# A second pass with column sums as column tiles, six convolution banks, a set GpSimd order and earlier weight widening

## The chip, the cores and the metric

The kernel runs on one core of a Trainium2 chip. The time is that of one execution on the device, in microseconds (us). The core has five engines that run side by side and wait for each other by semaphores: TensorE (PE, with its weight loads shown as PEld), VectorE (DVE), ScalarE (ACT), GpSimd (POOL) and SyncE (SP), which here issues the DMA transfers. Matrix products are written into PSUM[...]; the other working memory is SBUF.

## The reference

Two layers run over x of shape (8, 256, 64, 64), all in 32-bit floats.

```python
# layer 0: attention of all pixels over keys and values from a 4x4-strided convolution
xr = layernorm_over_channels(conv(x, w_sr, stride=4))
q, (k, v) = w_q @ x, split(w_kv @ xr)
x = x + gamma_s * (w_out @ softmax(q k^T / sqrt(32)) v)          # 8 heads
# layer 1: linear attention over qkv and over a 5x5 depthwise + grouped 8x8 of it
qkv = w_qkv @ x
agg = grouped(w_pw, depthwise5x5(qkv, w_dw))
ms = concat(qkv, agg)                                            # 64 heads of q, k, v with 8 rows
q, k, v = relu(ms.q), relu(ms.k), pad(ms.v, 1.0)                 # a column of ones beside v
kv = k^T v                                                       # per head: 8 x 9
out = q kv;  out = out[:8] / (out[8] + 1e-15)
x = x + batchnorm(w_proj @ out)
```

The ninth column of kv, made by the column of ones, is the sum of k over all pixels. These sums are the "column sums of k" of the title.

## The kernel before

Three passes follow each other in one program. The first pass does layer 0 and the qkv product and stores its results in HBM by planes. The second pass, with which this document deals, does for layer 1 the convolution of q and k and the products k^T v. The third pass divides, projects and adds.

**Units.** The second pass (`second_pass`) runs over 64 units u = (t, k, b): two halves t of the channels, four groups k of 32 channels, eight images b. The depthwise convolution and the small grouped product are one: `factors` loads two factors of the weights (wd and ws) and adds some of them up; `widened_k` and `widened_q` multiply them out into the matrices that PE uses. For k the convolution is done in three parts (`convolve`, i = 2, 0, 1), each of 16 pairs of weight load and product with the full 128x128 array, into one bank tagged cv. `paired` makes their inputs from d, as differences of columns; part 2 has a plain copy on POOL. For q, two units are done together, in nine products (`product`) after `across` and `down` have made differences of columns (c) and rows (y). An even unit does four of the nine, the odd unit after it five. `down` does half of each y on DVE and half on POOL.

**Products.** `summed_raw(u)` multiplies the raw k of unit u (kq) with v; 32 columns of weights at a time, so that four column tiles of the array work side by side on the four 32-partition groups of one bank (tag raw). `summed(p)` does the same for the convolved k of the unit before, p = u - 1, with 288 columns of v at its nine shifts (tag sums); DVE then weighs them with the taps and adds them up (p, kv, mixed, m).

**Column sums.** `reduced` adds up k over its eight parts on POOL in three steps, 512, 256 and 128 columns wide, into red_raw or red_agg. A matmul of one column then adds over the partitions: the reduced k is loaded as full 128x128 weights, and a column of ones runs through. For the raw k this is line 1482, in the raw bank. For the convolved k it is line 1494, in a bank of its own (tag few), called at the end of the unit (`ended`). Each of these is two pairs of load and product in the profile[...]. DVE copies the column beside the other sums, and SP stores both.

**Banks.** cv has five of PSUM's eight banks, raw, sums and few one each. A bank of cv is given back when DVE or ACT has read it.

**Order.** The tile framework sets the order on each engine by a simulation, by priority (the order in which the program text issues instructions) among what is ready in it. `tc.keep_in_program_order` nails one instruction behind the one that was issued before it on its engine. At run time each engine takes its instructions in that order. In the second pass the weight copies and the relu of kq on ACT and most stores on SP are nailed. The instructions of POOL are not, nor those of PE.

**Widening in portions.** The multiplying out of weights is a list of small steps (`chores`), worked off by `do(n)` at fixed places of a unit: before the q products, before convolution part 0, before raw, before convolution part 1 and at the end. The q weights of a group are made in two sets of 18 steps: one on DVE, one on POOL, 16 on ACT (line 613). This happens in the units with b = 1 and 2, called wide here; the first set is used from b = 2 on. Those of k are 32 steps on ACT (line 592), from b = 3 on.

**Start.** Before the loop come `positive(0)` (relu of the first kq on ACT, red_raw of unit 0 on POOL), the loading of the first q factors and the inputs of the first convolution.

The loop's own order for one unit u is: stores; differences of q (even u); convolution part 2; steps; q products; steps; part 0; q products; steps; raw and sums; column sum of raw; steps; part 1; the loads of d for u + 2; column sum of the convolved k; q products; relu of the next kq; steps.

## Time and profile before

| what | value |
|---|---|
| median of three runs | 3558.71 us (3556.86 to 3560.86) |
| the profiled execution | 3560.51 us; span of its instructions 3558.6 us |
| instructions | 91293 |
| L1372, convolution of k on PE | 3072 products, 385.7 us busy |
| L1403, q products on PE | 1536 with y, 512 with c, 256 with d |
| L1458, sums on PE | 4096 products, 265.8 us busy |
| L1441, raw on PE | 4096 products, 49.5 us busy |
| L1482 and L1494, column sums on PE | 128 products each, 24.5 and 18.4 us busy |
| L1352 to L1354, reduction on POOL | 64 each of red_raw and red_agg, 1.3, 0.8 and 0.5 to 0.7 us each |
| L613, widening of q on ACT | 256 copies, 0.34 us each |
| PE's idle time between 1960 and 2961 us | 23.5 us |
| DMA | 647 MB; from 1985 to 2800 us 260 GB/s |

Lines are those of the kernel before, and times within a trace count from the span's start. In the lines of the profile a group is named by line, engine, operation and tiles (out<-in), with "128*32" for the rows and columns of the array that a matmul uses. In the view in order of time the first two numbers are start and length in us, and a bracket at the end tells how long the engine was idle before and for whom it waited. A line of the waits reads: who, for whom, us in total, times, the longest. The view of stages gives for each stretch its length and then, for each engine, busy time and instructions. Busy times of PE are modelled where products overlap, so the starts of weight loads are the better measure of its pace. "issue" stands for a wait that the profile attributes to nobody.

### The profile page before, as it was taken

The page shows a single profiled execution, that of the slowest core. Times are in us where ns is not written, and L with a number is a line of the kernel's source. Part 1 is how long each engine was busy: PE and PEld are TensorE (multiplying, and loading weights), DVE is VectorE, ACT ScalarE, POOL GpSimd, SP SyncE. Part 2 cuts the span into 40 slices and gives each one's busy share as a digit, 9 for nine tenths or more (in the row PEclk, how much of TensorE's full clock was granted, in tenths as well). Part 3 has the DMA queues.
Part 4 walks back from the last instruction along what each step waited for, and adds up shares of the span by engine and source line. Part 5 has one row for each costly group of instructions (what it writes and reads, how often), then busy time and mean ns, then how long its engine had stood idle before and what let it go on. Part 6 is the DMA issues. An engine that isn't in the chain of part 4 may idle for free.

```text
span 3558.6 us, 91293 instructions
## 1 busy us (share of the span) xinstructions
PE 3481.9 (98%) x38050; PEld 2111.5 (59%) x38050; DVE 2278.5 (64%) x3499; ACT 1478.1 (42%) x3385; POOL 1858.6 (52%) x1762
## 2 busy tenths in 40 slices
PE   8999999999999999999998999999999999999998
PEld 5554655545545555455445888888888863333333
DVE  1567476575674766756777777777777774544442
ACT  2345354453453544545553344444444423333322
POOL 3557465565574655655763566555656532222222
PEclk9999999999999999999999999999999999999999
DMA  5446445455364454553646999999899987877873
GB/s 174 114 107 164 125 102 170 115 140 150 101 169 121 104 168 115 141 149 104 176 114 180 260 260 259 266 262 257 251 264 259 270 238 204 239 225 220 233 213 90
DMA packets 577191, 647.26 MB, mean 182 GB/s; under 512 B 81664, under 2 KB 452864, under 8 KB 576768
## 3 DMA queue, kind: packets, MB, share of 16 engines
q1 hardware_dynamic: 576768, 641.34, 64.7%
q8 instruction: 300, 4.92, 0.6%
q14 instruction: 123, 1.01, 0.1%
HBM read 389.85 MB, written 249.23 MB: 180 GB/s over the span
## 4 chain that ended last, share of the span: by engine, by line
PE 88%; DMA 5%; DVE 3%; ACT 1%; POOL 1%; issue 1%; SPq 1%; POOLq 0%; DVEq 0%; ACTq 0%
PE qkv L994 16%; PE p L1799 11%; PE cv L1372 8%; PE sc L847 8%; PE av L879 7%; PE cv L1403 6%; PE o L947 6%; PE q L829 6%; PE sr L750 6%; PE sums L1458 6%; PE rep L1785 2%; DMA raw<-planes 2%; PE av L905 2%; PE raw L1441 1%; PE den L1766 1%; DMA vq<-v 1%
## 5 line engine op out<-in xcount | busy, mean ns | idle before, releaser
L860 ACT ACTIVATE e<-sc 128x512 f32<-128x512 f32 x1024 | 528.4, 604 | 508.9 <-PE sc L847 508.9
L899 POOL TENSOR_TENSOR ef<-ef,e 128x512 f32<-128x512 f32 x512 | 687.8, 1353 | 91.4 <-ACT e L860 68.3
L892 POOL TENSOR_TENSOR ef<-e 128x512 f32<-128x512 f32 x256 | 329.3, 1305 | 544.6 <-ACT e L860 544.5
L1809 POOL TENSOR_TENSOR y<-z,xs 128x512 f32<-128x512 f32 x128 | 165.5, 1302 | 460.8 <-ACT z L1807 460.8
L1372 PE MATMUL cv<-w,c 128*128 128x128 f32 x3072 | 385.7, 279 | 6.3 <-DVE stage L1007 4.0
L1372 PEld LDWEIGHTS cv<-w,c 128*128 128x128 f32 x3072 | 363.1, 194 | 7.7 <-issue 4.1
L847 PE MATMUL sc<-q,kk 32*64 32x256 f32 x8192 | 298.5, 387 | 5.6 <-ACT e L860 5.2
L994 PE MATMUL qkv<-differences,combined 128*128 128x512 f32 x576 | 288.7, 592 | 0.6 <-POOL differences L964 0.6
L926 DVE STREAM_TRANSPOSE rden<-av 128x256 f32<-128x256 f32 x256 | 99.8, 428 | 283.2 <-ACT att L917 235.8
L1458 PE MATMUL sums<-vq,r 128*32 128x288 f32 x4096 | 265.8, 408 | 0.4 <-issue 0.4
L1799 PE MATMUL p<-raw,wp 128*128 128x512 f32 x512 | 248.8, 608 | 9.0 <-ACT z L1807 8.9
L1389 ACT ACTIVATE r<-s 128x512 f32<-128x512 f32 x128 | 80.9, 632 | 413.3 <-DVE s L1388 408.4
L879 PE MATMUL av<-e,vv 64*32 64x256 f32 x8192 | 252.4, 379 | 0.0
L847 PEld LDWEIGHTS sc<-q,kk 32*64 32x64 f32 x8192 | 155.4, 131 | 162.9 <-issue 101.4
L750 PE MATMUL sr<-x,wsr 128*128 128x256 f32 x1024 | 235.6, 382 | 8.7 <-DMA wsr<-in_w_sr_dram 8.6
L829 PE MATMUL q<-x,wq 128*128 128x512 f32 x512 | 241.9, 594 | 0.0
L1799 PE MATMUL p<-agg,wp 128*128 128x512 f32 x512 | 241.1, 593 | 0.0
L750 PEld LDWEIGHTS sr<-x,wsr 128*128 128x128 f32 x1024 | 194.8, 191 | 64.4 <-issue 38.2
L947 PE MATMUL o<-att,wout 128*128 128x512 f32 x512 | 230.3, 592 | 0.0
L932 DVE TENSOR_TENSOR att<-att,rall 128x512 f32<-128x512 f32 x128 | 217.9, 1702 | 4.4
L1010 DVE TENSOR_TENSOR whole<-part,qkv 128x512 f32<-128x512 f32 x256 | 172.3, 683 | 65.9 <-ACT part L1060 49.2
L837 ACT COPY q<-q 128x512 f32<-128x512 f32 x128 | 75.9, 593 | 317.4 <-PE q L829 317.4
(163 smaller groups left out, 6095.8 us busy)
## 6 DMA issues: line engine op xcount, KB each, us to landing
planes<-stage SPq DMA_DIRECT2D x128, 578.0 KB
d<-planes SPq DMA_DIRECT2D x128, 578.0 KB
vq<-v SPq DMA_DIRECT2D x256, 256.0 KB
raw<-planes SPq DMA_DIRECT2D x64, 578.0 KB
x<-in_xp_dram SPq DMA_DIRECT2D x64, 512.0 KB
wsr<-in_w_sr_dram SPq DMA_DIRECT2D x128, 256.0 KB
x<-x SPq DMA_DIRECT2D x128, 256.0 KB
k<-turned SPq DMA_DIRECT2D x256, 128.0 KB
```

What stands on the lines that cost most here:

```text
L750: nc.tensor.matmul(ps[:, oc], w[:, ci, oc * P : (oc + 1) * P], strips(b, f // 2)[:, ci, f % 2 * NK : (f % 2 + 1) * NK], start=(f == ci == ...
L829: nc.tensor.matmul(ps, consts["wq"][:, ci, c * P : (c + 1) * P], strips(b, s)[:, ci], start=(ci == 0), stop=(ci == 1),)
L847: nc.tensor.matmul(scs[h][HALVES[half], QH[kq % 2]], kks[b][rows, c, kq * P // 2 : (kq + 1) * P // 2], qs[rows, QH[half]], start=True, sto ...
L860: nc.scalar.activation(e[:, h % 2].rearrange("p q n -> p (q n)"), scs[h], AF.Exp, scale=D0**-0.5)
L879: nc.tensor.matmul(sums["av"][half][cols, : QB // 2], vvs[b][rows, kq, c * P + h * D0 : c * P + (h + 1) * D0], es[h // 2][rows, h % 2, kq ...
L892: tc.keep_in_program_order(nc.gpsimd.tensor_tensor(f, e[:, :, 0], e[:, :, 1], ALU.add))
L899: tc.keep_in_program_order(nc.gpsimd.tensor_tensor(f, f, e[:, :, half], ALU.add))
L947: nc.tensor.matmul(ps, consts["wout"][:, c, oc * P : (oc + 1) * P], att[c], start=(c == 0), stop=(c == 1))
L994: nc.tensor.matmul(ps, w, x, start=True, stop=True)
L1372: nc.tensor.matmul(ps[:, g * P : (g + 1) * P], c[:, g, cols], w[:, g, n * P : (n + 1) * P], start=(da == 0), stop=(da == 1),)
L1458: nc.tensor.matmul(ps[h * D0 : (h + 1) * D0, : 36 * D1].rearrange("p (r n e) -> p r n e", r=3, e=D1), kt[:, par, h, 2 * r + c], vq[:, r : ...
L1799: nc.tensor.matmul(as_block(ps, i // 2), wp[:, i, oc * P : (oc + 1) * P], block(g, i // 2, i % 2, j), start=(i == 0), stop=(i == 3),)
```

## The change

The column sums are made otherwise. `counted` takes the reduced k in four parts of 32 columns, each to its own column tile of the array, and writes one column per 32 partitions into the bank where the products of the same k already are: column 32 of raw, column 288 of sums. Both are issued one behind the other right after `summed`. The bank few goes away, and cv has six banks. DVE copies the raw sums and their column in one instruction. The work of DVE behind sums moves from `summed` to `ended`, behind the columns.

red_agg of unit p is issued earlier in the text (`reduced_agg`, ahead of convolution part 2 of the next unit). All instructions of POOL in the second pass are nailed: reductions, the copy of part 2, the POOL halves of y, the POOL step of widening.

The steps of widening are done at three places in place of five: 3, 3 and 13 in a wide unit (before 3, 3, 3, 6 and 9), 2, 2 and 4 in others (before four times 2). The last place is ahead of raw. `positive(0)` moves behind the first q factors and the inputs of the first convolution.

```diff
--- before.py
+++ after.py
@@ -600,12 +600,14 @@
     nc = tc.nc
     n = w.shape[1]
     for g in (2, 3):
-        (nc.vector if g == 2 else nc.gpsimd).tensor_tensor(
+        made = (nc.vector if g == 2 else nc.gpsimd).tensor_tensor(
             w[:, :, g].rearrange("p n (o f) -> p n o f", o=D1),
             wd[:, g].unsqueeze(2).to_broadcast([P, n, D1, R * R]),
             ws[:, g].unsqueeze(1).unsqueeze(3).to_broadcast([P, n, D1, R * R]),
             ALU.mult,
         )
+        if g == 3:
+            tc.keep_in_program_order(made)
         yield
     for g in (0, 1):
         for o in range(D1):
@@ -1225,8 +1227,10 @@
     )
     psums = {
         tag: ctx.enter_context(tc.tile_pool(name=f"psum_{tag}", bufs=1, space=bass.MemoryType.PSUM))
-        for tag in ("cv", "raw", "sums", "few")
+        for tag in ("cv", "raw", "sums")
     }
+
+    pinned = tc.keep_in_program_order
 
     def bank(tag, name, bufs=1, n=512):
         return psums[tag].tile([P, n], F32, tag=tag, name=name, bufs=bufs)
@@ -1296,7 +1300,7 @@
         d0, d1, d2 = (d[:, :, :, i : i + NB - 1 : 2] for i in range(3))
         if i == 2:
 
-            nc.gpsimd.tensor_copy(v, d1)
+            pinned(nc.gpsimd.tensor_copy(v, d1))
         else:
             nc.vector.tensor_sub(v, d2 if i else d0, d1)
 
@@ -1322,7 +1326,7 @@
         v = y.rearrange("p i g (b y x) -> p i (g b) y x", b=2, y=NB // 2)
         c0, c1, c2 = (c[:, :, i : i + NB - 1 : 2] for i in range(3))
         nc.vector.tensor_sub(v[:, 0], c0, c1)
-        nc.gpsimd.tensor_tensor(v[:, 1], c2, c1, ALU.subtract)
+        pinned(nc.gpsimd.tensor_tensor(v[:, 1], c2, c1, ALU.subtract))
 
     load_cells(0)
     load_tokens(0)
@@ -1344,14 +1348,14 @@
     ones = const.tile([P, 1], F32, tag="ones", name="ones")
     nc.vector.memset(ones, 1.0)
 
-    kts, reds, raws, mraws, state, maggs = {}, {}, {}, {}, {}, {}
+    kts, reds, raws, mraws, state, maggs, sums = {}, {}, {}, {}, {}, {}, {}
 
 
     def reduced(u, what, t):
         r = mid.tile([P, 4, P], F32, tag=f"red_{what}", name=f"red_{what}_{u}", bufs=1)
-        nc.gpsimd.tensor_tensor(r, t[0], t[1], ALU.add)
-        nc.gpsimd.tensor_tensor(r[:, :2], r[:, :2], r[:, 2:], ALU.add)
-        nc.gpsimd.tensor_tensor(r[:, 0], r[:, 0], r[:, 1], ALU.add)
+        pinned(nc.gpsimd.tensor_tensor(r, t[0], t[1], ALU.add))
+        pinned(nc.gpsimd.tensor_tensor(r[:, :2], r[:, :2], r[:, 2:], ALU.add))
+        pinned(nc.gpsimd.tensor_tensor(r[:, 0], r[:, 0], r[:, 1], ALU.add))
         reds[u, what] = r[:, 0]
 
     def positive(u):
@@ -1364,7 +1368,7 @@
     def convolve(u, i):
         t, k, b = units[u]
         c, w = cells[u, i], wt[t, k]
-        ps = bank("cv", f"cv1_{u}_{i}", 5)
+        ps = bank("cv", f"cv1_{u}_{i}", 6)
         for g in range(4):
             for da in range(2):
                 n = 2 * da + i if i < 2 else 4 + da
@@ -1392,7 +1396,7 @@
     def product(m, i, j):
         t, k, b = units[2 * m]
         now, w = quad[m], wq[t, k, (i, j)]
-        ps = bank("cv", f"cv0_{m}_{i}{j}", 5)
+        ps = bank("cv", f"cv0_{m}_{i}{j}", 6)
         for g in range(4):
             out = ps[:, g * P : (g + 1) * P]
             if i == 1:
@@ -1447,6 +1451,14 @@
                 )
         raws[u] = ps
 
+    def counted(ps, at, red):
+        for j in range(4):
+            cols = slice(j * D0, (j + 1) * D0)
+            nc.tensor.matmul(ps[cols, at : at + 1], red[:, cols], ones, start=True, stop=True)
+
+    def reduced_agg(u):
+        kt = kts[u].rearrange("p q h (n e) -> p q h n e", n=4)
+        reduced(u, "agg", (kt[:, 0].rearrange("p h n e -> p n h e"), kt[:, 1].rearrange("p h n e -> p n h e")))
 
     def summed(u):
         kt, vq = kts.pop(u), vqs.pop(u)
@@ -1462,8 +1474,11 @@
                     start=(i == 0),
                     stop=(i == 7),
                 )
+        sums[u] = ps
+
+    def ended(u):
         t, k, b = units[u]
-        reduced(u, "agg", (kt[:, 0].rearrange("p h n e -> p n h e"), kt[:, 1].rearrange("p h n e -> p n h e")))
+        ps = sums.pop(u)
         p = small.tile([P, 36, D1], F32, tag="p", name=f"p_{u}", bufs=1)
         nc.vector.tensor_mul(p, ps[:, : 36 * D1].rearrange("p (n e) -> p n e", e=D1), taps[t][:, k])
         s = small.tile([P, D1], F32, tag="kv", name=f"kv_{u}")
@@ -1473,26 +1488,18 @@
         nc.vector.tensor_mul(x, mix[:, 4 * t + k], s.unsqueeze(1).to_broadcast([P, D1, D1]))
         m = small.tile([P, D1 + 1], F32, tag="m", name=f"m_{u}")
         nc.vector.tensor_reduce(m[:, :D1], x, AX.X, ALU.add)
+        nc.vector.tensor_copy(m[:, D1:], ps[:, 36 * D1 : 36 * D1 + 1])
         maggs[u] = m
 
     def ended_raw(u):
         t, k, b = units[u]
-        ps = raws.pop(u)
-        col = ps[:, 64:65]
-        nc.tensor.matmul(col, reds.pop((u, "raw")), ones, start=True, stop=True)
         m = small.tile([P, D0 + 1], F32, tag="mraw", name=f"mraw_{u}")
-        nc.vector.tensor_copy(m[:, :D0], ps[:, :D0])
-        nc.vector.tensor_copy(m[:, D0:], col)
+        nc.vector.tensor_copy(m, raws.pop(u)[:, : D0 + 1])
         mraws[u] = m
 
     def stored_raw(u):
         t, k, b = units[u]
         tc.keep_in_program_order(nc.sync.dma_start(kvd[b, t][:, k], mraws.pop(u)))
-
-    def ended(u):
-        col = bank("few", f"few_{u}")[:, :1]
-        nc.tensor.matmul(col, reds.pop((u, "agg")), ones, start=True, stop=True)
-        nc.vector.tensor_copy(maggs[u][:, D1:], col)
 
     def stored_agg(u):
         t, k, b = units[u]
@@ -1529,10 +1536,10 @@
         j = t + 2 * what
         parts[j, k] = factors(nc, kept if what else w_q, a, j, k, 6 if what else 9)
 
-    positive(0)
     load_factors(0, 0)
     for i in (2, 0, 1):
         paired(0, i)
+    positive(0)
     for u in range(n_all + 3):
         p, q = u - 1, u - 2
         now, was, conv = u < n_all, 0 <= p < n_all, 0 <= q < n_all
@@ -1553,6 +1560,8 @@
         if conv and u % 2 == 0:
             across(q // 2, 0)
             down(q // 2, 1)
+        if was:
+            reduced_agg(p)
         if u < 2:
             chores.append(weights_q(0, u))
         if now:
@@ -1575,7 +1584,7 @@
         if u == n_all:
             next(ahead)
         if u == n_all + 1:
-            ahead.send(lambda name: bank("cv", name, 5))
+            ahead.send(lambda name: bank("cv", name, 6))
         if conv and u % 2:
             down(q // 2, 2)
         products(u, 0)
@@ -1588,14 +1597,20 @@
             down(q // 2, 0)
             across(q // 2, 2)
         products(u, 1)
-        do(3 if wide else 2)
+        do(13 if wide else 4)
         if now:
             summed_raw(u)
         if was:
             summed(p)
         if now:
+            counted(raws[u], D0, reds.pop((u, "raw")))
+        if was:
+            counted(sums[p], 36 * D1, reds.pop((p, "agg")))
+        if now:
             ended_raw(u)
-            do(6 if wide else 2)
+        if was:
+            ended(p)
+        if now:
             convolve(u, 1)
         if u + 1 < n_all:
             paired(u + 1, 1)
@@ -1605,14 +1620,11 @@
             load_tokens(2)
         if was and p == n_all // 2 - 1:
             load_taps(1)
-        if was:
-            ended(p)
         products(u, 2)
 
         if u + 1 < n_all:
             positive(u + 1)
-        do(9 if wide else 0)
-    ahead.send(lambda name: bank("cv", name, 5))
+    ahead.send(lambda name: bank("cv", name, 6))
```

## The prediction

> **What bounds the kernel now.** I read the page first, then the stretch of the second pass (about 1927 to 2895 us) in the views of stages, of waits and of time. The page says that TensorE (PE) is busy 98% of the span, and that no other engine comes near; the DMA row is the one to watch beside it.

> ```profile
> PE 3481.9 (98%) x38050; PEld 2111.5 (59%) x38050; DVE 2278.5 (64%) x3499; ACT 1478.1 (42%) x3385; POOL 1858.6 (52%) x1762
> ...
> DMA  5446445455364454553646999999899987877873
> ...
> 1960.00:2961.00 1001.00, 977.48 (x13615) 835.78 (x13610) 749.42 (x1261) 415.15 (x881) 566.49 (x551) 0.99 0.92 258
> ```

> The third line is the stage view over the second pass: length, busy PE, weight loads, DVE, ACT, POOL, then granted clock, DMA share and GB/s. PE has 23.5 us of idle in 1001, weight loads fill 836, and DMA is at 0.92. So a microsecond less of PE work is a microsecond less of time, unless DMA stops it. The order of time shows what one unit's sums cost (weight loads alone):

> ```profile
> 2610.66 0.64 PEld L1441 LDWEIGHTS raw<-vq,kq 128*32 128x32 f32 x63
> ...
> 2611.21 3.57 PEld L1458 LDWEIGHTS sums<-vq,r 128*32 128x32 f32 x63
> 2615.24 0.30 PEld L1482 LDWEIGHTS raw<-ones,red_raw 128*128 128x128 f32 x2 [0.47 <-issue]
> 2615.46 1.87 PEld L1372 LDWEIGHTS cv<-w,c 128*128 128x128 f32 x16
> 2617.24 0.30 PEld L1494 LDWEIGHTS few<-ones,red_agg 128*128 128x128 f32 x2
> 2617.47 0.30 PEld L1403 LDWEIGHTS cv<-y,w 128*128 128x128 f32 x2
> ```

> The reader is to see three spacings: the 64 column-tile pairs of raw take 2611.21 - 2610.66 = 0.55 us (8.6 ns each); L1482 holds PE 0.22 us until the convolution's loads, L1494 0.23; and 0.47 us pass between the loads of sums and L1482. From one L1482 to the next the units take 14.32 and 15.05 us by turns, to 0.01 us, but for one unit in eight. What happens there is in the waits and at 2198 us:

> ```profile
> PE cv L1403 <- ACT w L613: 11.2, 7, 2.3
> PE few L1494 <- POOL red_agg L1354: 4.1, 1, 4.1
> ...
> PE cv L1372 <- DVE s L1388: 1.8, 1, 1.8
> ...
> 2196.53 1.03 ACT L1359 ACTIVATE kq<-kq 128x1024 f32<-128x1024 f32 x1
> ...
> 2197.47 0.81 ACT L613 ACTIVATE w<-wd,ws 128x64 f32<-128x64 f32 x3
> ...
> 2198.33 0.83 PEld L1403 LDWEIGHTS cv<-d,w 128*128 128x128 f32 x6 [1.60 <-ACT w L613]
> ...
> 2437.00:2443.80 6.80, 4.90 (x23) 4.61 (x23) 3.79 (x4) 4.41 (x11) 5.83 (x7) 0.50 0.76 230
> ```

> Seven times PE waits for the last three of 16 weight copies on ACT, which stand behind the next unit's relu (kq). The last line shows the granted clock at 0.50 after two such idles in a row (1.8 and 1.9 us)[...].

> [...] No column tile with one column is in this trace, so I price it as raw's tile of 32. [...] the trace has 0.50 after 2437 and 2563 us, after idles of only about 2 us. [...]

> **The change, part by part.** The sum is made against the profiled execution, 3560.5 us (span 3558.6); the median of the runs is 1.8 lower.

> 1. Column sums. Removed per unit: L1482 0.22 and L1494 0.23, 0.45 us. Added: two times four products of two pairs each, 16 pairs at 8.6 ns = 0.14 us, right behind sums, so in the same tiling. The 0.47 us is mostly the last 288-column products running out: raw, with 32 columns, needs 0.04 from its last load to a full-array load (at 1933.7 us). A part of the new pairs' loads therefore lies in that 0.47. Between the last load of sums and the convolution there are 0.47 + 0.22 = 0.69 us now; I expect 0.47 + 0.14 + 0.04 = 0.65. Gain 0.04 + 0.23 = 0.27 per unit, times 64 = 17.3 us, taken as 17. Bounds: all 16 pairs hidden, 0.36 (23 us); pairs at 12 ns[...], 0.20 (13 us). DVE saves one copy of 0.15 us per unit, which is hidden: it is busy some 11.8 of 15 us.
> 2. Weights sooner. All 18 pieces of a wide unit are now ahead of raw, so the last three no longer stand behind kq; ACT works them off under the 4.6 us of raw and sums (13 x 0.34 = 4.4 us at most; measured spacing 0.26). Five stalled units take 16.00 instead of 14.32 us, 5 x 1.67 = 8.4; the one ending at 2448.96 takes 20.73 (6.4 more, with 1.8 for a bank and half clock), the one ending at 2570.82 18.69 (4.4 more). Together 19.1 us. Late next is the DVE widening (1.24 us) in these units, ahead of the copies that free banks; I leave 1.6 us to it and take 17.5. Bounds: 10 (if the bank wait and the clock drops stay) to 19.
> 3. The sixth bank. Its one visible stall (1.8 us on s, because DVE waited 2.35 us for a load of d) is in the 19.1. Nothing more is counted; PE waits for no other bank in this pass.
> 4. GpSimd in fixed order. POOL is busy 566 of 1001 us. An even unit's queue is now: y from d (2.7, waits for the load of d), red_agg (1.3 + 0.7 + 0.5), copy of c 0.7, perhaps the widening 1.3, y 1.3, red_raw 2.5. Behind a late d stand red_agg, whose column sum PE now needs 2.2 us sooner, and c. At 2612.7 d was in; y ended at 2615.4; r is there at 2620.0, so red_agg would end at 2622.6 and PE asks at 2629.3: 6.7 us to spare. Zero in the steady part. SP's queue gets nothing new; only the store of m waits for a copy behind the same column.
> 5. The start. positive(0) now comes behind the first copy of c, and that copy behind the first pass's last clearing of a stage (ends 1926.2), just before PE's first convolution at 1926.9: nothing. But POOL's first widening, run at 1950.5, now stands ahead of red_raw of unit 1 (run at 1940.1) and red_agg of unit 0 (1937.5). Its factors are issued at 1937.4 to 1939.3; if DVE takes them at 1941 (2.0 us with both engines busy), POOL is through by 1941 + 2.0 + 1.3 + 2.6 + 2.6 = 1949.5, where PE asks at 1944.1: up to 5.4 us, of which a convolution can fill 1.9. Against that goes the wait of 4.1 for few, and the half clock after it. I take a gain of 1; bounds -8 to +5.
> 6. The third pass takes the same bank by another count: zero.

> Sum: 17 + 17.5 + 1 = 35.5 us; 3560.5 - 35.5 = 3525 for a profiled run, 3523 for the median.

> **The rivals.** (a) DMA becomes the bound. For it: share 0.92, and 0.95 from 2760 to 2880 us; at 14.43 instead of 14.90 us per unit it would be 0.95 throughout. Against it: PE waits for DMA only 0.7 us, and 2420 to 2435 shows 1.04. If it holds at 0.94, the pass gains 1 - 0.92/0.94 = 2.1% of 1001, 21 us: 3538. (b) Slower: the fixed POOL order. Decisive where y from d ends more than 6.7 us later than at 2615.4: then red_agg holds PE in the 32 even units, and a stall of 2 us each costs 64 us: 3559 - 35 + 64 = 3588. For it: POOL waits 69.7 us for d, once 11.4. Against: with d that late PE would be waiting for y itself already. (c) The one-column tiles don't run side by side: 16 x 0.11 us (the duration of a 32-column load) = 1.76 per unit, 84 us lost, 3625; slower from 0.72 us per unit on. Raw, with the same tiles, speaks against. (d) The scheduler, which may move PE's work, puts the column sums behind the convolution[...]; some 0.2 per unit, 3527, within the forecast.

> **How the numbers follow.** Forecast with (d) 0.74; (a) 0.12; gains eaten by the start and DMA, no change, 0.04; (b) 0.07; (c) 0.03. About 0.2%, 7 us, can be told from no change. Faster 0.86, same 0.04, slower 0.10. Range: the forecast's terms run from 13 + 10 - 8 = 15 to 23 + 19 + 5 = 47 gained, 3544 to 3512; with 3 us on either side, 3509 to 3547, it holds (a) too.

> **What would show it.** Right: units of 14.05 and 14.78 us by turns, no longer one in eight; loads of the column sums, 128*32, within 0.7 us between sums and the convolution; no wait on w L613; clock 1.00 from 2000 to 2800 us. Wrong: PE waiting for red_agg, red_raw or d in even units; more than 0.3 us from the first load of the column sums to the last; a DMA share over 0.95 with PE idle beside it; DVE's s late by the widening, with PE waiting for it.

## The result, and the profile after

The changed kernel takes 3594.56 us (median of four runs, 3591.53 to 3604.05), and the kernel before, on the same chip, 3558.78 us. The ratio is 1.0102, with a 95% interval of 1.0084 to 1.0120: 36 us slower, where 35 us faster had been forecast. On another chip, in the last series below, it was 1.0103 (1.0080 to 1.0127).

The stage view over the second pass answers to the one shown of before (length, busy PE, weight loads, DVE, ACT, POOL, granted clock, DMA share, GB/s):

```profile
1960.00:2961.00 1001.00, 937.90 (x14360) 824.95 (x14360) 721.01 (x1189) 404.59 (x884) 571.90 (x556) 0.98 0.89 251
```

PE's idle time has grown from 23.5 to 63.1 us, and the DMA share has fallen from 0.92 to 0.89: DMA is not what holds PE. The waits of PE between 1927 and 2895 us tell for whom (who, for whom, us in total, times, the longest):

```profile
PE cv L1407 <- POOL y L1329: 50.5, 29, 3.0
PE raw L1457 <- POOL red_raw L1358: 6.4, 1, 6.4
PE cv L1376 <- DVE stage L1009: 4.0, 1, 4.0
PE sums L1457 <- POOL red_agg L1358: 2.6, 1, 2.6
```

The waits for w (11.2 us before) and few (4.1 us) are gone, as meant. In their place stands a wait that the kernel before does not have: the q products wait for POOL's half of y in almost every even unit. One such unit in the order of time, weight loads alone:

```profile
2271.80 3.57 PEld L1470 LDWEIGHTS sums<-vq,r 128*32 128x32 f32 x63
2275.45 0.37 PEld L1457 LDWEIGHTS raw<-ones,red_raw 128*32 128x32 f32 x6
...
2275.75 0.16 PEld L1457 LDWEIGHTS sums<-ones,red_agg 128*32 128x32 f32 x6
2275.93 1.86 PEld L1376 LDWEIGHTS cv<-w,c 128*128 128x128 f32 x16
...
2285.87 0.97 PEld L1407 LDWEIGHTS cv<-y,w 128*128 128x128 f32 x8 [1.67 <-POOL y L1329]
...
2291.16 0.37 PEld L1457 LDWEIGHTS raw<-ones,red_raw 128*32 128x32 f32 x6
```

Two things are to be seen. The column tiles do what they should: from their first load to the convolution's are 0.48 us, and nothing comes behind the convolution any more. But from 2275.45 to 2291.16 are 15.71 us, with 1.67 us of standing still; the odd unit ahead of it takes 14.70 us. POOL and ACT in the same stretch show where y comes from:

```profile
2281.67 1.31 POOL L1356 TENSOR_TENSOR red_raw<-kq 128x512 f32<-128x512 f32 x1 [7.15 <-ACT kq L1363]
2283.05 0.74 POOL L1357 TENSOR_TENSOR red_raw<-red_raw 128x256 f32<-128x256 f32 x1
2283.87 0.46 POOL L1358 TENSOR_TENSOR red_raw<-red_raw 128x128 f32<-128x128 f32 x1
2284.28 1.54 POOL L1329 TENSOR_TENSOR y<-d 128x512 f32<-128x512 f32 x1
```

```profile
2278.74 0.63 ACT L1393 ACTIVATE r<-s 128x512 f32<-128x512 f32 x1 [2.79 <-DVE s L1392]
2279.97 0.69 ACT L1413 ACTIVATE r<-side 128x512 f32<-128x512 f32 x1 [0.60 <-DVE side L1435]
2280.56 1.03 ACT L1363 ACTIVATE kq<-kq 128x1024 f32<-128x1024 f32 x1
```

Read backwards: PE goes on at 2285.87, when y (2284.28 to 2285.82) is there. y itself waited for nothing but its turn: ahead of it in POOL's queue stands red_raw, and red_raw waits for the relu of kq, which ACT takes in its own order behind two results of the convolutions. POOL was idle for 7.15 us, with y's input lying ready (DVE had made its own half of this y from the same d at 2269.24 to 2271.05 us), because the head of its queue was not. In the kernel before the scheduler had put y on POOL well ahead of where PE needs it, and red_raw of the same unit 11 us behind y:

```profile
2612.72 2.68 POOL L1325 TENSOR_TENSOR y<-d 128x512 f32<-128x512 f32 x1 [3.04 <-DMA d<-planes]
...
2623.98 1.31 POOL L1352 TENSOR_TENSOR red_raw<-kq 128x512 f32<-128x512 f32 x1
```

There y ends at 2615.40, and PE loads its weights at 2623.89. POOL's waits, first before and then after, show how the change turned many short waits with a purpose into one wait at the head of the queue:

```profile
POOL red_agg L1352 <- ACT r L1389: 138.2, 36, 7.1
POOL y L1325 <- PE cv L1403: 78.1, 20, 6.6
POOL y L1325 <- DMA d<-planes: 69.7, 23, 11.4
```

```profile
POOL red_raw L1356 <- ACT kq L1363: 363.6, 59, 12.8
POOL w L603 <- DMA vq<-v: 15.6, 1, 15.6
```

The last line is the second loss, at the start of the pass:

```profile
1956.87 1.56 POOL L603 TENSOR_TENSOR w<-wd,ws 128x512 f32<-128x512 f32 x1 [15.59 <-DMA vq<-v]
...
1961.35 0.46 POOL L1358 TENSOR_TENSOR red_raw<-red_raw 128x128 f32<-128x128 f32 x1
...
1964.27 0.45 POOL L1358 TENSOR_TENSOR red_agg<-red_agg 128x128 f32<-128x128 f32 x1
```

POOL stands 15.59 us in front of the first widening, and the two reductions behind it make PE wait 6.4 and 2.6 us. (The view names a DMA of v. The widening reads wd and ws, and DVE finished its sums of wd at 1956.79, 0.08 us before it began.)

**Where the time went.** From landmarks in the two traces (the pass's first run of convolution loads, the last load of sums in each unit, the end), after minus before:

| stretch | us | made of |
|---|---|---|
| up to the first convolution | +10.0 | PE, DVE, ACT and SP have the same instructions in the same order there, and on POOL only a copy of c and the first red_raw come later; over the thirteen traces of this study the load of the last product of the first pass (total) starts between 1922.5 and 1932.5 us, these two traces are its ends, and a second trace of the changed kernel has 1923.9. Not counted as the change's |
| start, six units | +9.0 | the waits above |
| 52 units in the middle | +16.0 | stalls of even units +53.4 (their length over 13.97 us, so with the slower clock after some of them, see the last section); column sums 52 x 0.35 = -18.2; units with widening -19.1 |
| last units of the pass | +4.4 | stalls on y: 4.0 us for POOL's half, 1.9 for DVE's |
| third pass | -4.4 | not followed up |

Without the first pass this is 25 us in this trace; in the second trace of the same kernel, in the last series, it is 44. The medians, 36 and 39 us, lie between.

### The profile page after: what moved, and what is told of

Its sections match the earlier page's. It is cut to its first block, busy times and chain, and to the rows that moved or that the text cites. A ratio compares the mean times of both kernels' runs of the same rounds, so it can differ in the third digit from the quotient of the medians.

```text
span 3593.6 us, 92668 instructions
## 1 busy us (share of the span) xinstructions
PE 3473.8 (97%) x38818; PEld 2111.5 (59%) x38818; DVE 2255.0 (63%) x3435; ACT 1477.1 (41%) x3385; POOL 1862.8 (52%) x1762
## 4 chain that ended last, share of the span: by engine, by line
PE 84%; POOL 4%; DMA 3%; DVE 3%; SPq 2%; ACT 2%; issue 1%; POOLq 0%; DVEq 0%; ACTq 0%
PE qkv L996 16%; PE p L1811 11%; PE sc L849 8%; PE av L881 7%; PE o L949 6%; PE sr L752 6%; PE q L831 6%; PE sums L1470 6%; PE cv L1376 5%; PE cv L1407 5%; PE rep L1797 2%; POOL y L1329 2%; PE av L907 2%; PE den L1778 1%; PE raw L1445 1%
## 5 line engine op out<-in xcount | busy, mean ns | idle before, releaser
L1356 POOL TENSOR_TENSOR red_raw<-kq 128x512 f32<-128x512 f32 x64 | 83.2, 1300 | 379.7 <-ACT kq L1363 379.7
L1407 PE MATMUL cv<-y,w 128*128 128x128 f32 x1536 | 203.1, 279 | 55.2 <-POOL y L1329 53.3
L752 PE MATMUL sr<-x,wsr 128*128 128x256 f32 x1024 | 238.3, 386 | 11.2 <-DMA wsr<-in_w_sr_dram 11.1
L1407 PEld LDWEIGHTS cv<-y,w 128*128 128x128 f32 x1536 | 186.8, 194 | 62.2 <-POOL y L1329 58.9
```

What stands on the lines that cost most here:

```text
L752: nc.tensor.matmul(ps[:, oc], w[:, ci, oc * P : (oc + 1) * P], strips(b, f // 2)[:, ci, f % 2 * NK : (f % 2 + 1) * NK], start=(f == ci == ...
L1407: nc.tensor.matmul(out, w[:, g], x, start=True, stop=True)
```

## The experiments

Theory T is what the traces suggest: not GpSimd's work, and not the earlier widening, but the place of red_raw in the fixed order, ahead of y from d, and its wait for the relu. Rival R1: the widening moved ahead of raw makes ACT, and so the relu, late. Rival R2: the column sums are asked of POOL too early. The chips of the experiments scatter more than the first (the kernel before alone: 3549 to 3578 us over the three series), so ratios are compared, and lengths of units.

### First series: what the order costs, alone and taken away

The changed kernel with POOL's order left to the scheduler:

```diff
-        pinned(nc.gpsimd.tensor_tensor(r, t[0], t[1], ALU.add))
+        nc.gpsimd.tensor_tensor(r, t[0], t[1], ALU.add)
...
-        pinned(nc.gpsimd.tensor_tensor(v[:, 1], c2, c1, ALU.subtract))
+        nc.gpsimd.tensor_tensor(v[:, 1], c2, c1, ALU.subtract)
```

(and so for the other reductions, the copy of c and the widening).

> The changed kernel without its fixed order of GpSimd, all else kept. Theory T (the fixed order puts red_raw of an even unit, which waits for the relu of kq, ahead of y from d, and PE waits for y): the PE waits on y L1329 (53.3 us in the changed kernel) go, units take about 14.0 and 14.7 us by turns, and the time is about 3525 us (3594.6 less some 70). Rival R1 (the widening of weights moved ahead of raw delays the relu on ACT): the order on GpSimd is not the cause, PE still waits about as long, 3580 us or more. Rival R2 (column sums asked earlier than GpSimd can deliver them): PE now waits for red_agg or red_raw L1358 at the column sums in many units, 3560 us or more.

Measured: 3538.41 us, ratio 0.9926 (0.9907 to 0.9944). No wait for POOL's y is among PE's ten largest in the second pass, and the units take 13.97 and 14.70 us by turns. R1 and R2 fall: earlier widening and column tiles are both in this kernel, and red_raw holds PE for only 3.5 us in all. POOL in an even unit, where PE loads this y's weights at 2285.74 (the first line is red_raw of the unit before):

```profile
2268.94 1.27 POOL L1354 TENSOR_TENSOR red_raw<-kq 128x512 f32<-128x512 f32 x1
...
2272.97 1.58 POOL L1327 TENSOR_TENSOR y<-d 128x512 f32<-128x512 f32 x1
...
2287.08 1.31 POOL L1354 TENSOR_TENSOR red_raw<-kq 128x512 f32<-128x512 f32 x1
```

y ends at 2274.55, 11 us before it is needed, and red_raw of the same unit comes 14 us behind it.

The changed kernel with the fixed order kept and only red_raw's place in it altered:

```diff
     def positive(u):
...
+    def reduced_raw(u):
+        kq = kqs[u]
...
         if conv and u % 2 == 0:
             across(q // 2, 0)
             down(q // 2, 1)
+        if now:
+            reduced_raw(u)
         if was:
             reduced_agg(p)
```

> The changed kernel with its fixed order of GpSimd kept, but the three additions of red_raw issued behind y from d of the even unit (and ahead of red_agg) instead of in front of it. Theory T: what costs is the place of red_raw alone; the waits on y L1329 go, red_raw and red_agg end some 3 us before PE asks, about 3525 us. A rival to T by which any fixed order costs (POOL then waits at one head of its queue or another, and delays copy c or y by turns): 3560 us or more. R1: as the changed kernel, about 3590.

Measured: 3541.97 us, ratio 0.9926 (0.9902 to 0.9949). The waits for POOL's y are gone. So a fixed order as such is not what costs; one group of three instructions in the wrong place does. POOL still waits 315 us for kq in this kernel, almost as long as in the changed one, and PE does not wait for it: what counts is what stands behind the wait. PE waits here 8.9 us for red_agg, in eight units, and 6.4 us for red_raw at the start.

The kernel before with the fixed order alone, in the order of its own text:

```diff
-        nc.gpsimd.tensor_tensor(v[:, 1], c2, c1, ALU.subtract)
+        tc.keep_in_program_order(nc.gpsimd.tensor_tensor(v[:, 1], c2, c1, ALU.subtract))
...
```

> The kernel before with nothing but the fixed order of GpSimd, in the order of its own text (red_raw of the next unit at the end of a unit, then y from d, red_agg behind the sums). Theory T: PE waits for y L1327 in about 30 even units, some 1.7 us each, with further stalls at few L1496, since red_agg then stands last: 3610 to 3650 us. R1 and R2 (the other parts of the change are needed for the stall): within 10 us of 3559.

Measured: 3614.00 us, ratio 1.0138 (1.0119 to 1.0157), 52 us lost, with PE waiting 46.9 us for y L1327 in 30 units. The order needs no other part of the change to do its damage. The further stalls expected at few were not there (0.9 us in all).

The column tiles and the sixth bank alone:

> The kernel before with the column tiles and the sixth bank alone: GpSimd in the scheduler's order, weights widened at the old places. From the unit lengths of the changed kernel without its stall the column sums bring 0.35 us a unit, 22 us: about 3537 us, with the waits on w L613 (11 us) still there. By the working of the forecast (0.27 us a unit): 3541 or 3542. R2 (PE asks GpSimd too soon for the column sums): waits on red_agg L1358, 3559 or more.

(its edit is the diff of the change without the fixed order, the earlier portions of widening and the move of `positive(0)`; red_agg keeps its earlier place in the text). Measured: 3551.33 us, ratio 0.9963 (0.9943 to 0.9984): 13 us by the ratio, less than either number expected. Its units are as short as foreseen, 13.97 and 14.70 us. But six units with widening now take about 4.1 (one 2.6) us more than their neighbours, where the kernel before has 1.67 in most of them:

```profile
PE cv L1405 <- ACT w L613: 14.0, 6, 2.4
```

Two things make up the 4.1 us. The wait itself is 2.3 to 2.4 us in all six units, where it is 1.4 in five units of the kernel before: the shorter unit seems to reach the same late weights sooner. And after the wait the granted clock drops in five of the six, and not in the one that takes 2.6 us more:

```profile
2082.70:2086.10 3.40, 3.37 (x17) 3.37 (x18) 1.35 (x2) 2.06 (x6) 3.32 (x5) 0.56 0.78 252
2555.60:2559.00 3.40, 3.38 (x67) 3.26 (x70) 2.29 (x4) 2.21 (x7) 3.32 (x5) 1.00 0.99 303
```

In those five units of the kernel before the clock stays at 1.00. So in these units the two gains depend on each other; the times can't show it, being 13 us here and 12 for the weights alone below, and 17 to 26 for both together.

### Second series: weights, banks, and the relu

The earlier widening alone, in the kernel before:

```diff
-        do(3 if wide else 2)
+        do(13 if wide else 4)
         if now:
             summed_raw(u)
...
-            do(6 if wide else 2)
...
-        do(9 if wide else 0)
```

> The kernel before with nothing but the earlier widening of the weights (GpSimd in the scheduler's order, the column sums as they were). By the forecast the wait on w L613 goes and eight or so units with widening lose most of their 19.1 us of excess over their neighbours: 17.5 us less than before. By what those units still cost in the kernel without the fixed order (0.6 to 1.2 us each, waits on y of DVE): about 12 us less. By a theory that the earlier widening belongs to the loss: not faster.

Measured: 3548.99 us, ratio 0.9967 (0.9955 to 0.9980): 12 us. Units with widening now exceed their neighbours by 0 to 1.5 us.

The changed kernel without the fixed order and with five convolution banks:

```diff
-        ps = bank("cv", f"cv1_{u}_{i}", 6)
+        ps = bank("cv", f"cv1_{u}_{i}", 5)
...
```

> The changed kernel without the fixed order of GpSimd and with five convolution banks instead of six. By the forecast (PE waits for no bank in the steady part) within 3 us of the same kernel with six banks, whose ratio to before was 0.9926. By a theory that the shorter units need the sixth bank: waits of cv on DVE's s or part or ACT's both, and 5 us or more slower than with six.

Measured: 3544.59 us, ratio 0.9950 (0.9935 to 0.9964). Against the first ratio with six banks this is 9 us worse, against the second one below (0.9951) it is the same. PE waits for DVE's s four times, 2.9 us in all. A gain from the sixth bank can't be told from nothing here.

The kernel with y ahead of red_raw, with the widening left to the scheduler:

```diff
-        if g == 3:
-            tc.keep_in_program_order(made)
```

> The changed kernel with red_raw issued behind y from d, and the widening alone left to the scheduler on GpSimd. Its sister with the widening fixed too kept some 12 us of stalls that the kernel in the scheduler's order has not: 6.4 for red_raw at the start, behind a widening that waits for its factors, and 8.9 for red_agg in units with a widening. If these come from the fixed place of the widening: about 12 us faster than the sister, ratio about 0.989 to before. If they come from red_raw being issued late: as the sister, 0.9926.

Measured: 3546.72 us, ratio 0.9957 (0.9942 to 0.9973), no better than its sister; a miss. The scheduler put the first widening in the same place, POOL again stood 15.3 us before it (PE then waited 7.5 us for red_raw), and PE waited 11.0 us for red_agg in ten places. To free one instruction in a row of fixed ones changed little; the start is right only where the reductions are free as well.

The sharpest test of T: POOL's order untouched (the two traces have the same sequence), the relu issued sooner on ACT.

```diff
+        if u + 1 < n_all:
+            positive(u + 1)
         if now:
             convolve(u, 1)
...
-        if u + 1 < n_all:
-            positive(u + 1)
```

> The changed kernel, GpSimd's fixed order untouched (red_raw stands ahead of y from d as before), but the relu of the next unit's kq is issued ahead of the last convolution and so ahead of its r on ACT, some 3 us sooner. Theory T (y is late only since red_raw ahead of it waits for that relu): the waits on y L1329 go or fall below 15 us and the time falls by 40 us or more from the changed kernel's, ratio to before below 1.0. A rival by which GpSimd's work itself is too long in the unit (red_raw, 2.6 us, in front of y, whenever it begins): the waits stay near 50 us and the ratio at 1.01.

Measured: 3552.23 us, ratio 0.9974 (0.9965 to 0.9983), with

```profile
PE cv L1407 <- POOL y L1329: 11.1, 9, 1.9
```

and most units at 13.97 and 14.70 us. red_raw still stands ahead of y, takes its time ahead of y, and in most units does no harm:

```profile
2279.87 1.29 POOL L1356 TENSOR_TENSOR red_raw<-kq 128x512 f32<-128x512 f32 x1 [8.03 <-ACT kq L1363]
...
2282.46 1.54 POOL L1329 TENSOR_TENSOR y<-d 128x512 f32<-128x512 f32 x1
```

Counted from the first load of the column sums (2278.06 us here, 2275.45 in the changed kernel) red_raw begins after 1.81 instead of 6.22 us, and y ends after 5.94 instead of 10.37. PE asks for it after 8.68 us in a unit without a stall (2286.74 here); 10.37 is 1.7 us too late, which is the stall, and 5.94 leaves 2.7 us to spare. Where POOL has more to do, as in units with widening, part of the stall is back (up to 2.2 us).

### Third series: the changed kernel and the best version again

The changed kernel unaltered, and the one without the fixed order, with more runs.

> The changed kernel itself, on the chip and beside the same runs of before as the next two: its ratio here is the measure for them. About 1.010.

Measured: 3600.09 us, 1.0103 (1.0080 to 1.0127).

> The changed kernel without the fixed order of GpSimd, once more, with more rounds: whether it is faster than before by its first ratio, 0.9926, or, like its five-bank sister, by 0.995. With the unit lengths of its trace (13.97 and 14.70 us for 14.32 and 15.05) the second pass alone gives 22 us, 0.994, and the weights 13 more, less some 5 lost where the passes meet: 0.9925.

Measured: 3541.98 us, 0.9951 (0.9935 to 0.9968): faster than both kernels, by 17 us rather than 26.

The same with the relu sooner, by the edit shown above:

> The changed kernel without the fixed order of GpSimd and with the relu of the next unit's kq issued ahead of the last convolution. If the relu's place on ACT costs only through the fixed order, as theory T has it: the same as without the fixed order alone, within 4 us. If red_raw's readiness also limits the free order: up to 10 us faster. If the relu ahead of r delays the sums: slower, with PE waiting for ACT r.

Measured: 3549.80 us, 0.9964 (0.9954 to 0.9974). In the free order the sooner relu brings no gain: what it cured was the fixed order's wait. It is 8 us behind by the medians, more than the 4 us that T allowed, and on the same chip 12 of its 19 runs are slower than the slowest of the ten without it. So it seems to cost something here. PE does not wait more for ACT's r than without it (1.4 us in both), and what the cost is stays open.

## Why the prediction was wrong, point by point

**The step that failed is number 4, "Zero in the steady part."** Its list of an even unit's queue began with y from d and ended with red_raw. In the text, `positive(u + 1)` stands at the end of the unit before, so with a fixed order red_raw of an even unit is ahead of y from d, and y gets red_raw's wait for the relu on top of its own for d: a term that the prediction put at nothing. Number 4 reasons by POOL working its queue off in order, and so it does in the changed kernel's trace, with 7.15 us of idleness in front of a ready y; what was wrong was the list. The question asked of the trace was whether a load of d could block red_agg; the question to ask was what each instruction waits for that now stands in front of another. The trace of the kernel before would have told: the red_raw at 2606.52 us, ahead of y at 2612.72, is that of the odd unit before, and the even unit's own stands at 2623.98, behind y. The list of signs of being wrong has waits for red_agg, red_raw and d, and none for y. The changed kernel shows 1.74 us of stall in a plain even unit and up to 3.9 in others, 53.4 us in the middle of the pass; without the fixed order or with red_raw behind y it goes, and with an earlier relu all but 11.1 us of waiting goes. Rival (b) had the engine, the size and the side right (3588 us, chance 0.07), but the wrong blocker, d, and the wrong victim, red_agg; that its 2 us a unit come near the 1.74 is luck. The argument against it ("with d that late PE would be waiting for y itself already") was sound for d and did not cover a new instruction in front of y.

**1, column sums:** the mechanism was right, the size too small. A unit is 0.35 us shorter (14.32 to 13.97, 15.05 to 14.70), not 0.27. The term that was off is what is left between sums and the convolution: 0.57 us (2275.36 to 2275.93), not 0.65. In the kernel before 0.47 us passed there ahead of L1482 with no pairs in it, so the sixteen new pairs and the way to the convolution add 0.10, where 0.18 had been counted. 64 units make 22 us, inside the bounds of 13 to 23. Rival (c), 1.76 us a unit for tiles one after the other, is far off: sixteen pairs add 0.10. In the sums, too, the four column tiles are seen to overlap: 64 products of 288 columns in 4.03 us (2611.21 to 2615.24 us in the kernel before), 63 ns each, where sixteen full-array products of 128 columns take 1.78 us (2615.46 to 2617.24), at which pace 288 columns would need about 250 ns (an estimate).

**2, weights:** the mechanism was right, the size too large. The wait on w is gone from the changed kernel's list; alone the edit is worth 12 us, not 17.5, within the bounds of 10 to 19. Units with widening in the kernel without the fixed order still cost 6.1 us over their neighbours in one trace and 13.9 in the other, where 1.6 had been left, by waits such as that for DVE's half of y (3.8 us, three times).

**3, the sixth bank:** no measurable gain, as forecast.

**5, the start:** wrong by more than its bound. The widening was expected to find its factors at 1941 us, which is 1951 in this trace, whose pass begins 10.0 us later; POOL waited for them until 1956.87. DVE, which was to take them at once, did its sums of wd from 1956.10 on, behind an s for which it had been idle for 5.81 us. To the sixth unit this pass lost 9.0 us, where the bounds were a loss of 8 and a gain of 5, and a gain of 1 was taken.

**6, and rival (a).** DMA did not become the bound of the pass: 0.95 from 2000 to 2400 us in the kernel without the fixed order, with PE busy 398.4 of 400. In one place it did, near the pass's end, where the third pass's first loads join in. There that kernel shows

```profile
PE cv L1405 <- DMA d<-planes: 3.0, 1, 3.0
```

```profile
2800.00:2810.00 10.00, 5.30 (x30) 3.93 (x28) 4.83 (x5) 2.02 (x4) 4.69 (x3) 0.83 1.08 313
```

with the DMA share at 1.08 and PE half idle; the unit takes 7.2 us more than its like, where in the kernel before the same unit takes 2.9 more. A part of the gain is handed back there.

Without its fixed order the changed kernel is 17 to 26 us faster than before, for a forecast of 35.5. In its better trace the second pass, up to the last sums, is 27.6 us shorter: column sums -20.3 (58 units of 0.35), widening -13.0, the start +1.4, the end of the pass about +4. What had been left out was not large in any one place: weights that still cost something, the start, and the end, where DMA is full.

## What to carry to other kernels

Before fixing the order of a helper engine, write down its queue as the text issues it, through the end of one iteration into the next, and for each instruction what it waits for and when that comes; then look at everything behind it. Here GpSimd waited 315 us for kq in the kernel with y ahead of red_raw, which took 0.9926 of the time before, and 363.6 us in the changed kernel, which took 1.0102; what differed was which instruction stands behind the one that waits. Two edits that both shorten the same unit are to be measured together and apart: here units that were 0.35 us shorter waited 2.3 us for late weights in place of 1.4, with the slower clock after most of these waits.

## What the runs showed of the hardware that was not expected

Eight loads of 128*32 with one moving column each for raw and for sums add only some 0.1 us between the last load of sums and the next full-array load: 0.57 us in all, against 0.47 us from the loads of sums to L1482 in the kernel before, where nothing lies between.

```profile
2035.40:2038.80 3.40, 0.70 (x6) 0.70 (x7) 3.23 (x3) 2.39 (x7) 3.32 (x4) 1.00 1.00 295
2038.80:2042.20 3.40, 3.40 (x89) 2.12 (x91) 1.82 (x2) 0.00 (x0) 3.24 (x5) 0.55 0.55 176
```

In the second stretch PE is busy throughout, at a clock of 0.55. What a lower clock costs shows in the eight weight loads of y behind a stall: from 2223.62 us they took 1.78 us at 0.51, and from 2285.87 us 0.97 us at 1.00. So this unit lost more than its wait: 3.4 us at 0.55 are 1.5 us lost (an estimate from the two figures), and with the stall's 2.96 that is near the 4.56 us by which the unit, at 18.53, is longer than an even unit without a stall. The length of the stall alone did not tell whether the clock dropped. In the same trace a stall of 3.09 us until 2006.42 left it at 1.00 (2006.4 to 2009.8), and one of 2.39 until 2223.62 brought 0.51 (2223.6 to 2227.0). In the kernel with the column tiles alone, five of six waits of 2.3 to 2.4 us were followed by a drop and one was not. What decides it was not found.
